# Tile 0's sums: two units joined onto others by VectorE, and queries of the last batch in other PSUM buffers

## The chip, the cores and the metric

The kernel runs on one core of a Trainium2 chip. Its engines run in parallel, each through its own queue of instructions in a fixed order: TensorE (matmuls, with PE and PEld as its rows in the profile: the matmuls and the weight loads), VectorE (DVE), ScalarE (ACT), GpSimd (POOL, which here also issues the gathers) and SyncE (SP, which issues plain transfers). The metric is the device time of one launch in microseconds, the median of several runs.

## The reference

One layer of graph attention over 16 batches of 1024 nodes with 512 features, float32 throughout. `adj` is a 1024 x 1024 matrix of zeros and ones, the same for all batches; a node attends to those nodes where its row is not zero.

```
h = jnp.maximum(_layernorm(x, axis=-1), 0.0)
q, k, v = (h @ W + b).reshape(b, n, 8, 64)      # for Wq, Wk, Wv
scores = jnp.einsum('bihd,bjhd->bhij', q, k) / 8 + where(adj == 0, -1e9, 0)
out = softmax(scores) @ v                       # per head
return x + out
```

Here the three projections are written as one line. Rows of `adj` differ much in how many ones they have: a few nodes have a great many neighbours, most have very few.

## The kernel before

**Tiles and units.** At the start the nodes are sorted by their number of neighbours and cut into 8 tiles of 128 nodes, so that all nodes of a tile have about as many. Tile 0 holds those with the most (11 slots each), tile 7 those with the fewest (2 slots). For every slot of a tile, a gather fetches one neighbour's K and V row for each of the 128 nodes into a ring of 23 places in SBUF (`gather`, line 1339 on GpSimd's queue; line 1337, on SyncE's, for a node's own row, which is plain). The slots of a tile are cut into units of up to four: `UNITS` lists 14 of them, as (tile, first slot, number of slots). Tile 0 has four: numbers 10 to 13, which are (0, 0, 4), (-1, 0, 4), (0, 4, 4) and (0, 8, 3). The second, with -1, holds pieces: further neighbours of the longest rows, spread over all 128 partitions; its queries are made by one matmul with the matrix `owner` (line 1326), and what it gives goes back to its rows through a matmul with `owner_t`.

**A unit's way.** VectorE multiplies K by the queries (line 1349) and reduces each head (1353); ScalarE takes the exponent (1357); V is multiplied by the weights, one slot on VectorE (1369) and the rest on ScalarE, head by head (1383, eight instructions a slot); then the slots of a unit are folded into the first (`fold`, 1388, on VectorE, some on GpSimd). Line numbers are those of the kernel before; the changed kernel's are some 10 higher.

**The sum over units.** In the tiles 1 to 7 the units of a tile are joined by VectorE (`join`, 1395). In tile 0 TensorE adds them up in PSUM (`add_up`, 1407: a matmul with the identity, or with `owner_t`; float32, two instructions a slot), but `PAIRED = (13,)` says that unit 13 is first joined onto unit 12 by VectorE. So TensorE sums the units 10, 11 and 12, each folded to one slot. VectorE then scales by the row sums (1443), `x` is added (1457) and GpSimd stores the rows (1460). The last batch is different: all its tiles but 7 are summed in PSUM, no slots are folded there, and it takes its tiles in another order (`LAST_ORDER`), tile 0 first.

**The rest of a batch.** Eight tiles of `x` are loaded, normalised (1087), turned by TensorE (1094, into the PSUM buffers `pht`), copied (1099), and projected (1105 the bias, 1107 the four matmuls, eight instructions): K and V into the PSUM buffers `pkv`, queries into `q`, two buffers of each kind. K and V are copied out and stored to HBM, from where the gathers of that batch read.

**What sets the order.** Every operation is listed with its engine, what it waits for and the buffers that it takes. `PLACES` gives each a number, by kind of batch (0, 1, 2, 3 for all the middle ones, next to last, last), and `ordered` puts each engine's queue in the order of these numbers, as far as buffers allow. A slot of the ring is given to a later gather when the last reader of what was in it is done (`touch` notes that reader).

Of the kernel before, what the change touches and what calls it, by code (L numbers as in the profile page):

```python
# [10 lines left out]
F32 = mybir.dt.float32  # L11
# [39 lines left out]
LAST_SHARES = (7, 6, 5, 4)  # L51
POOL_FOLDS = ((5, 0), (4, 0), (1, 0), (1, 4), (-1, 0))
# [67 lines left out]
        load_x=(31.049, 36.783, 44.902, 44.496, 48.208, 49.457, 50.746, 51.179,),  # L120
        norm=(67.626, 67.496, 74.201, 74.321, 77.427, 77.725, 77.636, 78.055,),
        flip=(54.462, 56.273, 60.803, 60.32, 67.659, 69.837, 67.669, 79.954,),
        unflip=(74.149, 74.341, 77.678, 77.688, 77.945, 88.353, 77.949, 88.373,),
        queries=(67.388, 82.797, 119.567, 126.815, 126.985, 142.131, 160.895, 166.215, 178.754,),
        gather=(79.658, 76.69, 82.341, 88.71, 96.247, 85.455, 130.077, 131.141, 97.49, 131.444, 131.207, 114.891,
# [3 lines left out]
        multiply=(44.958, 52.73, 91.409, 107.808, 127.369, 113.75, 131.901, 138.313, 148.456, 153.849, 160.505,  # L129
            168.689, 179.852, 179.155,),  # L130
        score=(44.978, 57.826, 94.048, 113.658, 128.337, 128.327, 144.151, 145.637, 148.577, 157.948, 166.105,
            172.449, 184.805, 190.24,),
        exponent=(110.192, 112.182, 112.945, 116.538, 127.025, 123.554, 131.068, 131.453, 148.261, 154.25, 165.903,
            171.356, 175.668, 179.424,),
        row_sums=(45.058, 64.344, 99.8, 117.62, 136.45, 158.731, 164.776, 202.291,),
        share=(52.255, 69.019, 106.586, 121.953,),
        weigh_v=(59.989, 136.42, 144.838, 146.315, 160.08, 162.684, 175.763, 179.21, 187.767,),
        weigh_s=(110.345, 112.764, 112.932, 112.883, 116.3, 116.059, 117.574, 119.959, 124.847, 119.535, 128.006,
            128.663, 128.577, 131.031, 143.069, 132.507, 147.11, 147.956, 133.383, 152.679, 153.798, 152.071, 165.883,
            155.205, 162.477, 175.658, 170.488, 167.365, 173.07, 174.582, 173.706, 178.014, 177.193, 176.615, 185.5,  # L140
            184.485, 184.518,),
        fold=(70.374, 102.858, 111.725, 138.272, 138.767, 136.852, 152.743, 144.2, 146.252, 146.283, 150.583, 159.412,
            156.722, 158.554, 164.711, 178.225, 172.057, 178.008, 186.564, 193.371, 186.442, 186.911, 194.742,
            203.514, 203.407, 203.544,),
        residual=(135.465, 136.054, 138.986, 147.406, 155.322, 174.928, 178.773, 223.099,),
        put_out=(135.561, 137.722, 153.06, 153.852, 172.277, 177.998, 210.259, 235.861,),
        join=(147.909, 162.67, 175.165, 205.718,),
        scale=(148.512, 165.374, 176.705, 210.064,),
        copy_q=(156.881,),
        add_up=(194.415, 206.93, 207.51,),  # L150
        more=(192.479,),
        pass_on=(194.778,),
        seen=(334.802,),
    ),
    1: dict(
        load_x=(-44.115, -43.713, -20.801, -33.74, -31.898, 35.921, 38.439, 40.768,),
        stats=(-68.353, -65.27, -59.298, -59.327, -16.301, -2.07, 22.869, 35.363,),
        norm=(-2.505, 0.857, 14.906, 21.095, 32.005, 25.638, 51.323, 59.514,),
        flip=(10.656, 11.218, 19.532, 62.497, 64.408, 64.772, 74.481, 81.456,),
        unflip=(1.813, 12.295, 17.709, 25.348, 35.031, 47.394, 57.982, 68.046,),  # L160
        proj_kv=(14.072, 17.322, 17.231, 42.55, 31.914, 64.021, 67.093, 64.398, 68.263, 71.481, 74.522, 77.094,
            77.939, 81.753, 84.619, 84.783,),
        evict_kv=(14.761, -27.097, 20.006, 23.587, 21.632, 43.531, 45.467, 32.738, 46.833, 59.822, 57.969, 60.522,
            69.174, 71.434, 72.595, 77.428,),
        store_kv=(7.044, 4.137, 13.698, 21.344, 43.631, 47.431, 47.421, 48.019,),
        variance=(-62.085, -59.298, 11.773, 41.168,),
        power=(-12.513, 19.605, 40.688, 54.482,),
        shift=(-59.504, -54.386, 26.781, 53.07,),
        queries=(94.739, 98.673, 106.104, 113.147, 115.672, 117.647, 123.411, 133.796, 173.926,),
        gather=(49.683, 84.791, 50.82, 87.832, 88.192, 50.603, 115.921, 116.04, 66.859, 116.49, 116.391, 116.11,  # L170
# [619 lines left out]
def pairs_up(b, B, u):  # L790

    return b < B - 1 and u in PAIRED

# [865 lines left out]
```

## Time and profile before

| | us |
|---|---|
| median of 3 runs | 1617.21 (1616.22 to 1619.01) |
| the profiled execution's own time | 1629.6 |
| its span, first to last instruction | 1627.9 |
| mean granted TensorE clock over the span | 0.987 |

The profiled execution is 12.4 us longer than the median. Times in a trace count from the span's start. A row of the timeline is a group of equal instructions on one engine; in square brackets stands how long the engine was idle before it and what ended that. VectorE and TensorE overlap the end of an instruction with the next, so what one costs is read from its start to the next one's start. The word "issue" means that the profile shows nothing that was waited for.

### The profile page before, as it was taken

How to read it: one execution, taken by the hardware profiler on the slowest of the kernel's cores; microseconds unless marked ns; L12 is line 12 of the kernel's file. 1: busy time of each engine (PE TensorE's matmuls, PEld its weight loads, DVE VectorE, ACT ScalarE, POOL GpSimd, SP SyncE). 2: the span in 40 equal slices, each digit the busy share in tenths (PEclk: the TensorE clock that was granted, in tenths of full speed). 3: DMA queues.
4: the chain of work that ended last, by engine and by line, in shares of the span. 5: the costliest groups of instructions: out<-in, count | busy, mean ns of one | idle time of the engine just before them, and what ended most of it. 6: DMA issues, size and time to landing. Idle time of an engine off the chain costs nothing.

```text
span 1627.9 us, 19217 instructions
## 1 busy us (share of the span) xinstructions
PE 1563.9 (96%) x4190; PEld 724.6 (45%) x4212; DVE 1531.8 (94%) x2090; ACT 1439.9 (88%) x5428; POOL 1275.3 (78%) x1185
## 2 busy tenths in 40 slices
PE   8889999999999999999999999999999999999688
PEld 4444444444444444444444444444444444444233
DVE  8679999999999999999999999999999999999897
ACT  4258989999998989899898989989899998989887
POOL 3766778788888888888888888888888878877785
PEclk9999999999999999999999999999999999999789
DMA  6487998999899998989999898999999899998895
GB/s 246 144 326 246 334 340 328 338 344 350 311 370 338 350 339 334 352 319 374 331 348 340 332 340 326 364 352 334 344 333 334 338 371 321 351 346 301 315 355 201
DMA packets 149875, 531.55 MB, mean 327 GB/s; under 512 B 19052, under 2 KB 19052, under 8 KB 149752
## 3 DMA queue, kind: packets, MB, share of 16 engines
q0 software_dynamic: 109840, 390.70, 65.8%
q1 hardware_dynamic: 39912, 139.56, 23.2%
q8 instruction: 35, 0.57, 0.1%
q14 instruction: 88, 0.72, 0.1%
HBM read 429.46 MB, written 100.72 MB: 326 GB/s over the span
## 4 chain that ended last, share of the span: by engine, by line
DVE 36%; ACT 15%; POOL 13%; issue 10%; PE 5%; DMA 3%; DVEq 0%; POOLq 0%; SPq 0%; ACTq 0%
ACT ring L1383 12%; DVE ring L1349 10%; DVE weights L1353 9%; DVE ring L1388 6%; POOL ring L1339 6%; PE acc L1407 2%; DVE st L1061 2%; POOL out_dram L1460 2%; POOL ring L1388 2%; PE pq L1107 2%; DMA ring<-kv,index 2%; DVE ring L1369 2%; POOL x L1457 1%; DVE ring L1395 1%; ACT kvt L1125 1%
## 5 line engine op out<-in xcount | busy, mean ns | idle before, releaser
L1383 ACT ACTIVATE ring<-ring,weights 128x64 f32<-128x64 f32 x4704 | 1155.0, 341 | 48.5 <-DVE weights L1362 24.5
L1339 POOL DMA_INDIRECT ring<-kv,index x608 | 650.1, 1069 | 183.1 <-issue 163.2
L1107 PE MATMUL pq<-wq,hT 128*128 128x512 f32 x1024 | 461.9, 594 | 0.7
L1107 PE MATMUL pv<-wv,hT 128*128 128x512 f32 x960 | 431.4, 592 | 0.9 <-ACT kvt L1125 0.9
L1107 PE MATMUL pk<-wk,hT 128*128 128x512 f32 x960 | 431.6, 592 | 0.6 <-ACT hT L1099 0.2
L1353 DVE TENSOR_REDUCE weights<-ring 128x32 f32<-128x2048 f32 (+2 forms) x224 | 423.0, 1894 | 1.2
L1349 DVE TENSOR_TENSOR ring<-ring,pq 128x2048 f32<-128x2048 f32 (+2 forms) x208 | 388.5, 1868 | 12.2 <-remote 6.4
L1107 PEld LDWEIGHTS pq<-wq,hT 128*128 128x128 f32 x1024 | 195.2, 191 | 225.6 <-issue 221.8
L1107 PEld LDWEIGHTS pv<-wv,hT 128*128 128x128 f32 x960 | 181.9, 190 | 216.0 <-issue 211.9
L1107 PEld LDWEIGHTS pk<-wk,hT 128*128 128x128 f32 x960 | 182.1, 190 | 207.9 <-issue 202.8
L1388 DVE TENSOR_TENSOR ring<-ring 128x512 f32<-128x512 f32 (+1 forms) x301 | 250.6, 845 | 6.0 <-issue 4.2
L1460 POOL DMA_INDIRECT out_dram<-x,perm x128 | 146.5, 1145 | 40.0 <-issue 24.1
L1052 POOL DMA_INDIRECT x<-in_x_dram,perm x128 | 133.1, 1039 | 36.2 <-issue 31.0
L1388 POOL TENSOR_TENSOR ring<-ring 128x512 f32<-128x512 f32 x90 | 116.1, 1291 | 5.9 <-DVE ring L1388 3.5
L1457 POOL TENSOR_TENSOR x<-x,o 128x512 f32<-128x512 f32 x64 | 81.9, 1280 | 23.1 <-DVE o L1443 21.9
L1087 ACT ACTIVATE h<-x,shift,rstd 128x512 f32<-128x512 f32 x120 | 94.2, 815 | 5.2 <-DVE shift L1077 4.3
L1357 ACT ACTIVATE weights<-weights 128x32 f32<-128x32 f32 (+2 forms) x224 | 48.7, 223 | 54.9 <-DVE weights L1353 51.9
L1369 DVE TENSOR_TENSOR ring<-ring,weights 128x512 f32<-128x512 f32 x143 | 95.4, 681 | 0.0
L1094 PEld LDWEIGHTS pht<-ident,h 128*128 128x128 f32 x512 | 62.9, 142 | 66.0 <-issue 52.6
L1099 ACT COPY hT<-pht 128x512 f32<-128x512 f32 x128 | 73.1, 574 | 14.1 <-remote 12.3
L1061 DVE BATCH_NORM_STATS2 st<-x 128x6 f32<-128x512 f32 x120 | 81.4, 679 | 2.7 <-DMA x<-in_x_dram,perm 2.7
L1094 PE MATMUL pht<-ident,h 128*128 128x128 f32 x512 | 74.6, 276 | 9.7 <-ACT h L1087 9.0
(241 smaller groups left out, 1115.1 us busy)
## 6 DMA issues: line engine op xcount, KB each, us to landing
ring<-kv SPq DMA_DIRECT2D x128, 512.0 KB
kv<-kvt SPq DMA_DIRECT2D x120, 512.0 KB
ring<-kv,index POOLq DMA_INDIRECT x608
ring<-in_adj_dram SPq DMA_DIRECT2D x8, 512.0 KB
x_first<-in_x_dram SPq DMA_DIRECT2D x8, 256.0 KB
x<-in_x_dram,perm POOLq DMA_INDIRECT x128
out_dram<-x,perm POOLq DMA_INDIRECT x128
wk<-in_L_gnn_Wk_dram SPq DMA_DIRECT2D x1, 1024.0 KB
```

The lines of the kernel that those rows point to most:

```text
L1052: nc.gpsimd.indirect_dma_start(out=X[n][:], out_offset=None, in_=x_rows, in_offset=on(ap=perm[:, t : t + 1], axis=0), element_offset=b * N * D
L1061: nc.vector.bn_stats(st, X[n])
L1094: nc.tensor.transpose(PH[n][:, c, :], hn[:, ts(c, P)], ident)
L1107: nc.tensor.matmul(pt, HT[n][:, c, :], W[name][:, c, :], start=(apart and c == 0), stop=(n != -NT and c == DC - 1))
L1339: nc.gpsimd.indirect_dma_start(out=G[i][:, s].rearrange("p j d -> p (j d)"), out_offset=None, in_=KV[b % len(KV)][:], in_offset=on(ap=inde ...
L1349: nc.vector.tensor_tensor(k, k, Q[b, t][:, None, :].to_broadcast([P, count, D]), ALU.mult)
L1353: nc.vector.tensor_reduce(weights[:, w, :], heads(G[i][:, :count, 0, :]), AX.X, ALU.add)
L1369: nc.vector.tensor_tensor(v, v, own.to_broadcast([P, n, H, HD]), ALU.mult)
L1383: nc.scalar.activation(v[:, h, :], v[:, h, :], AF.Identity, scale=weights[:, c + s, h : h + 1])
L1388: engine.tensor_tensor(v[:, 0:n], v[:, 0:n], v[:, first : first + n], ALU.add)
L1457: (nc.vector if residual_by_vector(b, B, t) else nc.gpsimd).tensor_tensor(rows, rows, add, ALU.add)
L1460: nc.gpsimd.indirect_dma_start(out=out_rows[t], out_offset=on(ap=perm[:, t : t + 1], axis=0), in_=X.pop(b * NT + TILES.index(t))[:], in_of ...
```

## The change

Three things change. `PAIRED` becomes a table: unit 10 is joined onto unit 12, and unit 12 onto unit 13, both by VectorE, in all batches but the last. TensorE then sums the units 11 and 13 only, so two in place of three. In the last batch queries of the tiles 0 and 1 go into the PSUM buffers of K and V, and those of the tiles 2 and 3 into the buffers of the turned tiles; before, all went into the two of `q`. And nearly all numbers in `PLACES` are new, apart from the setup and the first projections. A unit that is joined away keeps its first slot in the ring until that join, where unit 10's was free after its sum on TensorE.

```diff
+LAST_QUERIES = {0: 'pkv', 1: 'pkv', 2: 'pht', 3: 'pht'}
...
     3: dict(
...
-        join=(157.031, 175.397, 183.579, 209.406,),
+        join=(158.199, 174.732, 182.978, 204.245, 209.904,),
...
-        add_up=(196.008, 204.056, 216.943,),
+        add_up=(209.732, 226.555,),
...
-PAIRED = (13,)
+PAIRED = {10: 12, 12: 13}
...
-        q = ("q", b, t)
+        q = (bank_of(b, B, t), "q", b, t)
...
-        elif pairs_up(b, B, u):
-            add(("join", k), "DVE", weighed + earlier)
-            touch(k, [0], ("join", k))
-            touch(k - 1, [0], ("join", k))
-            plan.ops[plan.number["add_up", k - 1]][2].append(("join", k))
-            added = [("add_up", b * NU + v) for v in added_up(b, B, home)]
         else:
-            add(("add_up", k), "PE", weighed + ([before] if u != parts[0] else []), [acc])
+            for from_, ready in [one for one in paired if PAIRED[one[0] % NU] == u]:
+                add(("join", from_), "DVE", weighed + ready)
+                touch(from_, [0], ("join", from_))
+                touch(k, [0], ("join", from_))
+                weighed = [("join", from_)]
+            paired = [one for one in paired if PAIRED[one[0] % NU] != u]
+            if pairs_up(b, B, u):
+                paired = [(k, weighed)]
+                continue
+            sums_of = added_up(b, B, home)
+            add(("add_up", k), "PE", weighed + ([before] if u != sums_of[0] else []), [acc])
...
+def bank_of(b, B, t):
+
+    return LAST_QUERIES.get(t, "q") if b == B - 1 else "q"
...
-            Q[b, t] = ps_q.tile([P, D], F32, tag="q", name=f"pq_{b}_{t}")
+            bank = bank_of(b, B, t)
+            Q[b, t] = dict(q=ps_q, pkv=ps_kv, pht=ps_h)[bank].tile([P, D], F32, tag=bank, name=f"pq_{b}_{t}")
...
-            to = i - 1 if pairs_up(b, B, i % NU) else b * NU + parts_of(t)[0]
+            to = b * NU + (PAIRED[i % NU] if pairs_up(b, B, i % NU) else parts_of(t)[0])
```

Where it moves instructions is shown at two places. The first is tile 0's sum in a middle batch. On TensorE before (acc_0 is tile 0's sum; pk, pv, pq are projections of the tile whose number follows; pht a turned tile; p_more the pieces' row sums):

```order
L1107 MATMUL pv_7_8730<-wv,hT_7_8663 128x512 x4
L1407 MATMUL acc_0_8801<-ring,ident 128x512
...
L1107 MATMUL pv_6_8808<-wv,hT_6_8758 128x512 x4
L1422 MATMUL p_more_8816<-more_8702,owner_t 128x8
...
L1107 MATMUL pq_7_8819<-wq,hT_7_7864 128x512 x4
L1407 MATMUL acc_0_8801<-ring,owner_t 128x512
...
L1107 MATMUL pk_6_8897<-wk,hT_6_8758 128x512 x4
L1094 MATMUL pht_5_8907<-ident,h_5_8905 128x128 x4
L1407 MATMUL acc_0_8801<-ring,ident 128x512
```

and in the changed kernel, at the same place:

```order
L1117 MATMUL pv_7_8694<-wv,hT_7_8686 128x512 x4
...
L1117 MATMUL pv_6_8729<-wv,hT_6_8727 128x512 x4
...
L1117 MATMUL pq_7_8756<-wq,hT_7_7887 128x512 x4
L1433 MATMUL p_more_8802<-more_8764,owner_t 128x8
L1418 MATMUL acc_0_8831<-ring,owner_t 128x512
...
L1117 MATMUL pk_6_8868<-wk,hT_6_8727 128x512 x4
L1418 MATMUL acc_0_8831<-ring,ident 128x512
L1104 MATMUL pht_5_8913<-ident,h_5_8894 128x128 x4
```

The first sum is gone, the pieces' sum comes first, and the last sum stands straight behind a projection.

On VectorE at the same place before, from the fold of unit 13 ahead of tile 6's multiplication (L1349) to tile 0's scaling (L1443); L1395 is the join, L1353 the reduction to scores, L1429 a row sum:

```order
L1388 TENSOR_TENSOR ring<-ring 128x512
L1349 TENSOR_TENSOR ring<-ring,pq_6_8872 128x3x512
L1395 TENSOR_TENSOR ring<-ring 128x512
L1362 TENSOR_TENSOR weights<-weights,inv_7_8884 128x16
L1353 TENSOR_REDUCE weights<-ring 128x24
L1429 TENSOR_REDUCE sums_8882<-weights 128x8
L1433 RECIPROCAL inv_6_8926<-sums_8882 128x8
L1369 TENSOR_TENSOR ring<-ring,weights 128x512
L1362 TENSOR_TENSOR weights<-weights,inv_6_8926 128x24
L1443 TENSOR_TENSOR o_0_8930<-acc_0_8801,inv_0_8828 128x512
```

and now, from tile 7's reduction on (L1406 is the join, L1364 the reduction, L1399 a fold, L1380 the multiplication by weights):

```order
L1364 TENSOR_REDUCE weights<-ring 128x16
L1406 TENSOR_TENSOR ring<-ring 128x512
L1399 TENSOR_TENSOR ring<-ring 128x512
L1360 TENSOR_TENSOR ring<-ring,pq_6_8834 128x3x512
L1440 TENSOR_REDUCE sums_8899<-weights 128x8
L1444 RECIPROCAL inv_7_8901<-sums_8899 128x8
L1399 TENSOR_TENSOR ring<-ring 128x512
L1373 TENSOR_TENSOR weights<-weights,inv_7_8901 128x16
L1406 TENSOR_TENSOR ring<-ring 128x512
L1364 TENSOR_REDUCE weights<-ring 128x24
L1380 TENSOR_TENSOR ring<-ring,weights 128x512
L1440 TENSOR_REDUCE sums_8899<-weights 128x8
```

There are two joins for one, and tile 6's row sum (the last row) stands behind the multiplication by weights and not ahead of it.

The second place is the start of the last batch's attention. On TensorE before (pq_0, pq_1, pq_2 are the last batch's queries, acc_0_12797 the sum of the batch before, acc_0_12847 that of the last):

```order
L1107 MATMUL pq_0_12662<-wq,hT_0_12528 128x512 x4
L1422 MATMUL p_more_12668<-more_12660,owner_t 128x8
L1407 MATMUL acc_0_12797<-ring,ident 128x512
L1407 MATMUL acc_0_12797<-ring,owner_t 128x512
L1326 MATMUL pq_-1_12812<-q_15_12715,owner 128x512
L1407 MATMUL acc_0_12797<-ring,ident 128x512
L1407 MATMUL acc_0_12847<-ring,ident 128x512 x4
...
L1107 MATMUL pq_1_12852<-wq,hT_1_12496 128x512 x4
L1407 MATMUL acc_0_12847<-ring,owner_t 128x512 x4
...
L1107 MATMUL pq_2_12936<-wq,hT_2_12430 128x512 x4
```

and now:

```order
L1117 MATMUL pq_0_12708<-wq,hT_0_12476 128x512 x4
...
L1117 MATMUL pq_2_12742<-wq,hT_2_12423 128x512 x4
L1433 MATMUL p_more_12775<-more_12630,owner_t 128x8
...
L1117 MATMUL pq_1_12816<-wq,hT_1_12469 128x512 x4
L1337 MATMUL pq_-1_12822<-q_15_12714,owner 128x512
L1418 MATMUL acc_0_12854<-ring,owner_t 128x512
L1418 MATMUL acc_0_12854<-ring,ident 128x512
L1418 MATMUL acc_0_12902<-ring,ident 128x512 x4
L1418 MATMUL acc_0_12902<-ring,owner_t 128x512 x4
```

The queries of tiles 2 and 1 stand ahead of the last batch's first sum, where they stood behind it. On VectorE the same moment, before, from tile 0's first multiplication of the last batch to its score (L1353):

```order
L1349 TENSOR_TENSOR ring<-ring,pq_0_12662 128x4x512
L1388 TENSOR_TENSOR ring<-ring 128x512
L1429 TENSOR_REDUCE sums_12075<-weights 128x8
L1431 TENSOR_TENSOR sums_12075<-sums_12075,p_more_12668 128x8
L1433 RECIPROCAL inv_0_12765<-sums_12075 128x8
L1388 TENSOR_TENSOR ring<-ring 128x2x512
L1353 TENSOR_REDUCE weights<-ring 128x32
```

and now, from the row sums that stood in between:

```order
L1440 TENSOR_REDUCE sums_12084<-weights 128x8
L1442 TENSOR_TENSOR sums_12084<-sums_12084,p_more_12775 128x8
L1444 RECIPROCAL inv_0_12779<-sums_12084 128x8
L1399 TENSOR_TENSOR ring<-ring 128x512
L1360 TENSOR_TENSOR ring<-ring,pq_0_12708 128x4x512
L1364 TENSOR_REDUCE weights<-ring 128x32
```

The score follows its multiplication at once; the fold and the row sum stand ahead of both, the larger fold behind.

## Rows read from the trace of the kernel before

**Rows 1.** The page, part 1: busy us, share of the span, instructions, by engine.

```profile
PE 1563.9 (96%) x4190; PEld 724.6 (45%) x4212; DVE 1531.8 (94%) x2090; ACT 1439.9 (88%) x5428; POOL 1275.3 (78%) x1185
```

**Rows 2.** Timeline, TensorE: queries of tile 0's pieces, six batches apart.

```profile
743.79 1.02 PE L1326 MATMUL pq_-1_6152<-q,owner 128*128 128x512 f32 x2
...
1315.88 1.02 PE L1326 MATMUL pq_-1_10945<-q,owner 128*128 128x512 f32 x2
```

**Rows 3.** Stretches: from:to, length, busy us by engine, clock, DMA share, GB/s.

```profile
100.00:300.00 200.00, 192.76 (x516) 88.82 (x520) 188.60 (x260) 174.07 (x660) 145.06 (x137) 1.00 0.89 323
...
743.84:1315.93 572.09, 565.49 (x1521) 261.82 (x1526) 555.44 (x709) 532.83 (x2034) 472.54 (x427) 1.00 0.93 342
...
1507.58:1553.42 45.84, 25.48 (x56) 10.39 (x54) 39.11 (x38) 38.03 (x155) 32.89 (x28) 0.74 0.87 322
1553.42:1617.31 63.89, 63.89 (x150) 28.46 (x151) 57.94 (x64) 61.42 (x260) 45.39 (x45) 0.97 0.81 296
```

**Rows 4.** Waits, 743.84 to 1315.93: total us, times, longest.

```profile
DVE sums L1429 <- ACT weights L1357: 6.1, 6, 1.0
...
PE acc L1407 <- POOL ring L1388: 4.3, 6, 0.9
...
DVE shift L1077 <- POOL rstd L1073: 1.8, 3, 0.6
DVE ring L1395 <- POOL ring L1388: 1.7, 6, 0.3
DVE o L1443 <- issue: 1.6, 6, 0.3
```

**Rows 5.** Timeline, TensorE, tile 0's sum in a middle batch: start, length, instruction.

```profile
1063.74 1.13 PE L1407 MATMUL acc<-ring,owner_t 128*128 128x512 f32 x2 [0.91 <-POOL ring L1388]
...
1075.65 0.60 PE L1094 MATMUL pht<-ident,h 128*128 128x128 f32 x4
1076.08 1.02 PE L1407 MATMUL acc<-ring,ident 128*128 128x512 f32 x2
1076.94 0.38 PE L1105 MATMUL pq<-bias_parts,chosen 128*128 128x512 bf16 x1
```

**Rows 6.** Timeline, VectorE, the same batch.

```profile
1065.56 1.21 DVE L1349 TENSOR_TENSOR ring<-ring,pq 128x1024 f32<-128x1024 f32 x1
...
1072.34 0.68 DVE L1395 TENSOR_TENSOR ring<-ring 128x512 f32<-128x512 f32 x1
1072.94 0.16 DVE L1362 TENSOR_TENSOR weights<-weights,inv 128x16 f32<-128x16 f32 x1
...
1075.78 0.21 DVE L1429 TENSOR_REDUCE sums<-weights 128x8 f32<-128x32 f32 x1 [1.01 <-ACT weights L1357]
...
1077.14 0.69 DVE L1443 TENSOR_TENSOR o<-acc,inv 128x512 f32<-128x512 f32 x1 [0.27 <-issue]
...
1081.87 2.28 DVE L1349 TENSOR_TENSOR ring<-ring,pq 128x2048 f32<-128x2048 f32 x1
```

**Rows 7.** Timeline, SyncE's queue, the same batch: two tiles' own rows.

```profile
1064.89 0.80 SPq L1337 DMA_DIRECT2D ring<-kv  x2
```

**Rows 8.** The chain that ended last: a transfer of own rows, issue to landing.

```profile
1208.18 7.54 DMA ring<-kv
```

**Rows 9.** Timeline, TensorE, the last batch.

```profile
1553.42 6.33 PE L1407 MATMUL acc<-ring,ident 128*128 128x512 f32 x10 [8.83 <-ACT ring L1383]
1559.58 0.38 PE L1105 MATMUL pq<-bias_parts,chosen 128*128 128x512 bf16 x1
...
1563.23 3.60 PE L1407 MATMUL acc<-ring,owner_t 128*128 128x512 f32 x8
```

**Rows 10.** Timeline, VectorE, the last batch's first multiplication to the second unit's.

```profile
1543.48 0.69 DVE L1388 TENSOR_TENSOR ring<-ring 128x512 f32<-128x512 f32 x1 [2.65 <-issue]
...
1546.53 2.28 DVE L1353 TENSOR_REDUCE weights<-ring 128x32 f32<-128x2048 f32 x1
...
1549.93 2.28 DVE L1349 TENSOR_TENSOR ring<-ring,pq_-1_12812 128x2048 f32<-128x2048 f32 x1
```

**Rows 11.** Timeline, ScalarE, the last batch's first exponent.

```profile
1548.84 0.23 ACT L1357 ACTIVATE weights<-weights 128x32 f32<-128x32 f32 x1 [3.49 <-DVE weights L1353]
```

More of the change, by code (lines that the diff above doesn't have):

```diff
@@ L129 @@
[L129 to L147, printed above, removed]
@@ L154 @@
+        scale=(153.427, 160.007, 182.169, 221.914,),
+        copy_q=(160.489,),
+        add_up=(200.11, 204.453,),
+        more=(186.586,),
+        pass_on=(192.394,),
+        seen=(326.256,),
     ),
     1: dict(
[L156 to L159, printed above, removed]
@@ L167 @@
[L167 to L170, printed above, removed]
[3 rows of a table removed]
-        multiply=(99.447, 106.031, 113.782, 124.398, 147.886, 144.395, 150.08, 154.625, 164.449, 169.213, 169.369,
-            178.115, 183.375, 191.926,),
-        score=(103.818, 107.037, 121.82, 141.74, 149.288, 149.734, 154.724, 157.574, 167.151, 169.267, 170.491,
-            182.002, 191.719, 192.028,),
@@ new lines @@
+        power=(-27.83, 37.657, 53.519, 73.645,),
+        shift=(-62.679, -50.756, 16.305, 46.882,),
+        queries=(96.04, 97.197, 100.217, 100.298, 118.016, 118.026, 122.901, 129.472, 170.315,),
+        gather=(49.722, 85.439, 49.712, 92.725, 88.878, 40.197, 130.734, 119.12, 91.528, 131.17, 129.324, 130.801,
[3 rows of a table added]
+        multiply=(97.646, 105.465, 117.719, 136.145, 147.976, 147.737, 154.978, 156.653, 158.632, 169.388, 171.311,
+            184.95, 187.823, 191.374,),
+        score=(104.805, 108.124, 118.759, 140.985, 148.529, 149.443, 155.805, 157.452, 163.849, 171.275, 177.068,
+            186.685, 188.087, 192.312,),
@@ new lines @@
+        power=(-14.991, -10.265, 52.087, 75.445,),
+        shift=(-30.12, -10.7, 53.88, 71.152,),
+        queries=(91.566, 91.576, 95.948, 105.026, 137.748, 142.356, 153.47, 158.033, 178.403,),
+        gather=(79.888, 96.164, 80.341, 100.314, 104.174, 78.277, 116.916, 113.956, 80.484, 124.104, 116.979, 105.307,
[3 rows of a table added]
+        multiply=(100.961, 103.766, 117.132, 135.054, 138.706, 139.368, 143.565, 149.08, 159.633, 172.002, 176.008,
+            179.546, 182.64, 188.483,),
+        score=(101.009, 105.353, 128.377, 135.874, 142.578, 140.199, 151.469, 151.102, 162.118, 173.01, 176.394,
+            181.922, 183.495, 191.159,),
@@ new lines @@
+        power=(-16.248, 13.193, 24.813, 75.905,),
+        shift=(-17.537, 12.061, 24.405, 64.603,),
+        queries=(105.553, 114.967, 117.853, 134.981, 139.088, 142.596, 149.894, 152.407, 164.897,),
+        gather=(76.982, 100.773, 71.893, 102.244, 104.263, 71.941, 117.648, 105.093, 80.672, 118.798, 113.462,
[3 rows of a table added]
+        multiply=(102.859, 110.919, 120.256, 121.594, 127.606, 133.289, 137.421, 146.803, 158.772, 168.658, 175.921,
+            177.499, 182.661, 185.356,),
+        score=(108.79, 114.812, 121.35, 125.982, 136.236, 136.795, 145.913, 152.286, 162.65, 171.648, 176.816,
+            182.615, 185.052, 189.96,),
@@ L378 @@
+        more=(158.123,),
+        pass_on=(211.725,),
+        seen=(547.64,),
     ),
```

393 lines of the change are left out of this document (196 added, 197 removed), and 37 rows, old and new, of the table gather.

## The prediction

> **What bounds the kernel now.** I read the page's busy times first, then the stretches, the period of a batch, the waits, and the timelines at the two places that the change touches. The page alone shows four engines close to full [rows 1], so the stretch of even running decides. In it the single matmul of tile 0's pieces returns after 572.09 us for six batches, 95.35 us a batch [rows 2]. Over the same stretch TensorE is busy 565.49 us, VectorE 555.44, ScalarE 532.83 and the DMA engines 0.93 of the time, at the full granted clock of 2.4 GHz [rows 3]. By sixths: TensorE 94.25 us busy and 1.10 idle; VectorE 92.57 busy and 2.78 idle; ScalarE 88.81 busy. TensorE is the first limit and VectorE the second, with little between them.
>
> What is in the idle time? TensorE's has 0.72 us a batch before the sum of the pieces' unit, which waits for GpSimd's fold (4.3 us in 6 times); 0.38 is scattered. VectorE's has four waits that come back in most batches: 1.02 for an exponent ahead of a row sum, 0.30 for GpSimd's power, 0.28 for GpSimd's fold ahead of a join, 0.27 ahead of tile 0's scaling: 1.87 [rows 4]. The other 0.91 are gaps under 0.15 us, between most instructions, and I count them as part of its work.
>
> The end is another regime. From 1507.58 to 1553.42 us no engine is full (TensorE 25.48 of 45.84), at a mean clock of 0.74; from 1553.42 to 1617.31 TensorE is busy without a gap, ScalarE 61.42 of 63.89, VectorE 57.94 [rows 3].
>
> **The joined units, even running.** TensorE loses one sum of one slice, two matmul instructions: from 1076.08 to the next instruction at 1076.94, 0.86 us a batch [rows 5]. VectorE gains one join of 128x512: from 1072.34 to the next at 1072.94, 0.60 us [rows 6]. Nothing hides either, since both engines are full; so this is a trade, and the later of two sums counts:
>
> - TensorE: 94.25 - 0.86 = 93.39 us of work. The wait for GpSimd's fold stays: TensorE comes to it 0.86 earlier, but GpSimd's fold now stands ahead of a gather that it stood behind. With the old 1.10 idle: 94.49.
> - VectorE: 92.57 + 0.60 + 0.91 = 94.08 us of work and short gaps. Of its waits two should go by the order. Tile 6's row sum stood directly behind the reduction that its exponent needs, and waited 1.01 us [rows 6]; now a multiplication by weights stands between (0.60), and in ScalarE's new order one copy out of PSUM less is ahead of that exponent. Tile 0's scaling came 0.2 us after the last sum ended; now the sum can end before 1076 and a fold stands ahead of the scaling. The two waits for GpSimd, 0.58 together, I leave: 94.66.
>
> The last two cannot both be had without some new waiting between three queues that run in order, so I take 94.8, nearer to VectorE's 94.66 than to today's 95.35: 0.55 us a batch. From 300 us to 1507.58 are 12.7 batches, say 13: 7.2 us. The ends: no gain beyond TensorE's 0.86, that is 11.2 us; and at worst VectorE keeps all four waits: 94.08 + 1.87 = 95.95, a loss of 0.60 a batch, 7.8 us.
>
> **New waits of this part.** There are three. First, TensorE's last sum waits for the second join, behind which stand all projections of the next batch. On VectorE the join begins 6.78 us after tile 7's multiplication at 1065.56 now [rows 6]; the new order puts the added join and a small multiplication of weights ahead of it, 0.69 us, so it ends near 1073.7. TensorE reaches the sum near 1075.65 - 0.86 = 1074.8 [rows 5]: a reserve of 1.1 us, where today it is 3.1. From 1.1 us on TensorE stands, and from 1.9 on its saving is used up. Second, the first unit's slot of the ring stays taken until its join. Before, TensorE's sum of that unit freed it; tile 4's own rows of the next batch go there, and SyncE issued them with another tile's at 1064.89 [rows 7]. Now they wait for the first join, which by the order lies about midway between tile 7's multiplication and the second join, near 1069.7. Such a transfer took 7.54 us in the chain [rows 8]: landing 1077.2. The multiplication that needs it stands at 1081.87 today [rows 6], about 1081.2 then (0.60 more, two waits of 1.02 and 0.27 less). Cost nothing, with 4.0 us in hand. Third, the slot of the third unit comes free with its join near 1073.7 rather than with the sum at 1076.94, so the gather behind it on GpSimd's queue is freer than now.
>
> **The last queries.** Projections of tiles 2 and 1 move in front of the wait in which TensorE has little to do, since they need no buffer of the two that queries share. One takes from 1559.58 to 1563.23, 3.65 us [rows 9]; two are 7.3 us off the busy run from 1553.42. VectorE and ScalarE do not shrink with it. ScalarE has 2.47 us of idle time in that run [rows 3], so this alone can give at most about that. The order adds a thing: tile 0's first score of the last batch now stands straight behind its multiplication. Before, it stood behind folds of the batch before that waited 2.65 us and more [rows 10], and ScalarE stood 3.49 us for it [rows 11]. Ends for the last stretch: nothing, and 2.47 + 3.49 = 5.96. The gathers of the second unit still have to land, VectorE began it without a wait at 1549.93, so I take the middle, 3 us.
>
> **The new places elsewhere.** Nearly all places of all batches are new numbers, and the order is reshuffled by a few positions on each queue. In the first 300 us TensorE idles 7.24 us between 100 and 300 [rows 3]; half of that either way is my bound, and I take zero.
>
> **Sum.** 7.2 + 3.0 = 10.2 us. The profiled execution took 1629.6 us, with a span of 1627.9 and 1.7 around it: 1619.4. The median of the runs, 1617.2, lies 12.4 lower; less the same 10.2 it is 1607.0.
>
> **Rivals.**
>
> 1. VectorE eats the gain. Its waits shrink only to 1.26, then 94.08 + 1.26 is today's period; only the end gains: 1614. For it: VectorE has 0.91 less to spare than TensorE had. Against: the 1.02 us wait visibly loses its cause.
> 2. VectorE becomes the limit and keeps its waits, because the join ahead of the second fold pushes everything behind it and TensorE stands at its last sum: 95.95 a batch, 7.8 lost and 3 won, 1622. It decides at the second join of a batch, from about 1.9 us later than I place it.
> 3. Tile 4's own rows come late. It begins where the transfer takes over 11.5 us. One microsecond late makes VectorE's batch 95.66, 4 us in all, 1618; three late 1644. Against it: 7.54 in the row.
> 4. TensorE is not a limit at all, its busy time being that of overlapping instructions; then VectorE is, at 97 of 100, and each join costs its 0.60, fifteen of them 9.0, with nothing won at the end: 1626. Against it: matmuls start 0.43 us apart with no gap wherever the timeline is opened, and TensorE's waits are few [rows 4, 5].
>
> The Trainium skill, Perfetto Trace Analysis, section Identifying the Most-Contended Engine, speaks for this fourth case: it calls matmul busy time a poor measure of TensorE, because matmuls are pipelined, and would have the weight loads' share read instead, while VectorE's busy share is fair as it stands. By that rule TensorE has half its time free (weight loads 261.82 of 572.09 us [rows 3]) and the change loads the fuller engine: 1626. The trace does not bear that out, as a weight load of 0.17 us goes with each matmul of some 0.38 us, so that its share cannot pass about 46% here however full TensorE is.
>
> **Chances.** My forecast 0.61, its own range 1600 to 1613; the first rival 0.16; the second 0.12; the third 0.06; the fourth 0.05. A difference of 0.2%, 3.2 us, is what a measurement of this kernel can tell from none: faster means under 1614.0, slower over 1620.4. The first rival lies at the border and gives most of "same", with part of the third: 0.16. Slower takes the second, the fourth, the rest of the third and a little for places that I have not followed: 0.22. Faster: 0.62. The range runs from the best of both main terms with nothing from the start, 1617.2 - 11.2 - 5.96 = 1600, a microsecond lower for the start, to the second rival, 1622.
>
> **What would show it.** The period between the single matmuls of tile 0's pieces near 94.8 us; TensorE busy 93.4 a batch; VectorE 93.2 busy with under 1 us in waits over 0.15, and the row sum's wait gone. At TensorE's last sum of a batch no wait for VectorE's join. Between the last projection and the first sum of the last batch, three projections of queries and not one; ScalarE's 3.49 us gone. I am wrong if the period is 95.3 or more, if VectorE waits for rows of K and V in the middle of the run, or if the gain sits in the first 300 us.

## The result and the profile after

The changed kernel takes 1600.15 us, the median of 6 runs (1597.45 to 1602.04); the kernel before takes 1615.72 in the same comparison. The ratio is 0.9902, with a 95% interval of 0.9887 to 0.9917: 15.6 us (13 to 18) faster. The forecast was 10.2 us, in the right direction and too small.

The profiled execution after took 1597.45 us, 2.7 under its median, with a span of 1595.8. That of before lay 12.4 over its median. The two spans differ by 32 us, twice what the medians do, so no difference of whole spans is used here; stretches that start and end at the same instruction are. The busy times, to be read against [rows 1]:

```profile
PE 1548.5 (97%) x4151; PEld 719.2 (45%) x4182; DVE 1532.9 (96%) x2105; ACT 1437.5 (90%) x5428; POOL 1257.0 (79%) x1185
```

The period, from TensorE's timeline, by the same instruction and the same batches as [rows 2]:

```profile
726.30 1.02 PE L1337 MATMUL pq_-1_6123<-q,owner 128*128 128x512 f32 x2
...
1285.36 1.02 PE L1337 MATMUL pq_-1_10917<-q,owner 128*128 128x512 f32 x2
```

559.06 us for six batches: 93.18 a batch, where it was 95.35. The stretches that answer to [rows 3] (length, then busy us of PE, PEld, DVE, ACT, POOL, clock, DMA share, GB/s); the third row runs from the last batch's first query projection to 1.1 us ahead of the row with its first sum, the fourth from there to the end. The last two rows of [rows 3] have other ends, so their lengths are not to be compared with these:

```profile
100.00:300.00 200.00, 195.88 (x528) 90.31 (x530) 196.67 (x267) 181.37 (x690) 153.52 (x142) 1.00 0.92 331
726.34:1285.36 559.02, 557.86 (x1502) 260.31 (x1513) 547.40 (x715) 532.39 (x2039) 464.56 (x426) 1.00 0.96 350
1496.78:1523.40 26.62, 14.18 (x34) 5.86 (x32) 26.21 (x26) 25.28 (x105) 19.40 (x18) 0.79 0.90 331
1523.40:1595.80 72.40, 60.92 (x138) 25.81 (x139) 62.85 (x79) 60.73 (x258) 45.96 (x46) 0.92 0.71 271
```

In the even run TensorE stands 1.2 us in 559; before it stood 6.6 in 572. VectorE is busy 91.2 us a batch, 1.3 less than before, although it has a join more. The waits of that stretch (total, times, longest) are these, to be read beside [rows 4]: VectorE's, then TensorE's only one.

```profile
DVE x L1468 <- POOL ring L1399: 3.1, 6, 1.6
DVE shift L1087 <- POOL rstd L1083: 2.5, 4, 0.6
DVE ring L1360 <- PE pq L1117: 0.3, 1, 0.3
DVE o L1454 <- PE acc L1418: 0.2, 1, 0.2
```

```profile
PE pq_-1_6922 L1337 <- DVE ring L1360: 0.4, 1, 0.4
```

The waits for the exponent and for GpSimd's fold ahead of a sum or a join are gone, and so is that ahead of tile 0's scaling, but for one of 0.2 us. A wait for GpSimd's fold ahead of tile 4's residual (the addition of `x`) is new. Tile 0's sums in one batch on TensorE, and on VectorE from tile 7's multiplication to the scaling, answering to [rows 5, 6]:

```profile
1040.62 1.10 PE L1418 MATMUL acc<-ring,owner_t 128*128 128x512 f32 x2
...
1052.51 1.02 PE L1418 MATMUL acc<-ring,ident 128*128 128x512 f32 x2
```

```profile
1042.57 1.22 DVE L1360 TENSOR_TENSOR ring<-ring,pq 128x1024 f32<-128x1024 f32 x1
...
1046.27 0.68 DVE L1406 TENSOR_TENSOR ring<-ring 128x512 f32<-128x512 f32 x1
...
1050.14 0.69 DVE L1406 TENSOR_TENSOR ring<-ring 128x512 f32<-128x512 f32 x1
...
1053.01 0.20 DVE L1440 TENSOR_REDUCE sums<-weights 128x8 f32<-128x32 f32 x1
...
1054.18 0.69 DVE L1454 TENSOR_TENSOR o<-acc,inv 128x512 f32<-128x512 f32 x1
```

No bracket stands on any of them. The second join ends at 1050.83 and TensorE comes to its sum at 1052.51, 1.7 us later; I had placed 1.1.

Where did VectorE's 1.3 us come from? Two groups of small instructions hold it: the variance (L1070, after L1080) and the sharing out of the weights (L1362, after L1373). First before, from 743.84 to 1315.93, then after, six batches each (busy us, mean ns of one):

```profile
L1070 DVE TENSOR_SCALAR rstd<-mv 128x2 f32<-128x2 f32 x24 | 10.0, 417 | 0.0
L1362 DVE TENSOR_TENSOR weights<-weights,inv 128x24 f32<-128x24 f32 (+2 forms) x24 | 9.1, 377 | 0.4
```

```profile
L1080 DVE TENSOR_SCALAR rstd<-mv 128x2 f32<-128x2 f32 x24 | 4.7, 195 | 0.0
L1373 DVE TENSOR_TENSOR weights<-weights,inv 128x24 f32<-128x24 f32 (+2 forms) x24 | 4.4, 181 | 0.6
```

The same work costs 10.0 us less in six batches, 1.67 a batch. A mean hides the cause: of the 24 variances before, 18 took 0.14 us on average and 6, one a batch, 1.25. Each of the six stood beside GpSimd's fold and ended 0.04 us after it. One of them, VectorE's row, then GpSimd's:

```profile
1062.46 1.25 DVE L1070 TENSOR_SCALAR rstd<-mv 128x2 f32<-128x2 f32 x1
```

```profile
1062.41 1.27 POOL L1388 TENSOR_TENSOR ring<-ring 128x512 f32<-128x512 f32 x1
```

Of the 24 sharings before, 7 took 0.5 us or more, the others at most 0.26. Each of the seven stood beside an addition of `x` on GpSimd (L1457) and ended some 0.06 us after it:

```profile
1090.32 0.51 DVE L1362 TENSOR_TENSOR weights<-weights,inv 128x32 f32<-128x32 f32 x1
```

```profile
1089.48 1.29 POOL L1457 TENSOR_TENSOR x<-x,ring 128x512 f32<-128x512 f32 x1
```

In the new order no variance stands beside a fold on GpSimd and the longest took 0.30 us, the longest sharing 0.19. The Trainium skill, SBUF — State Buffer, section Who interferes with whom, names a pair of SBUF ports that VectorE and GpSimd share and that, for certain instructions, one of them holds for a whole instruction. These rows agree with that, a block to the end of GpSimd's instruction and not a slowdown.

The last batch, TensorE from its first query projection on, answering to [rows 9]; then ScalarE's first two exponents, answering to [rows 11], and the second of them before:

```profile
1496.78 0.38 PE L1115 MATMUL pq<-bias_parts,chosen 128*128 128x512 bf16 x1
...
1500.43 0.38 PE L1115 MATMUL pq<-bias_parts,chosen 128*128 128x512 bf16 x1
...
1504.21 0.38 PE L1115 MATMUL pq<-bias_parts,chosen 128*128 128x512 bf16 x1
...
1513.38 2.08 PE L1418 MATMUL acc<-ring,owner_t 128*128 128x512 f32 x2 [4.50 <-DMA ring<-kv,index]
1524.50 6.80 PE L1418 MATMUL acc<-ring,ident 128*128 128x512 f32 x10 [9.04 <-issue]
1531.14 3.63 PE L1418 MATMUL acc<-ring,owner_t 128*128 128x512 f32 x8
```

```profile
1518.44 0.23 ACT L1368 ACTIVATE weights<-weights 128x32 f32<-128x32 f32 x1 [1.06 <-DVE weights L1364]
...
1526.62 0.23 ACT L1368 ACTIVATE weights<-weights 128x32 f32<-128x32 f32 x1 [2.03 <-DVE weights L1364]
```

```profile
1555.55 0.23 ACT L1357 ACTIVATE weights<-weights 128x32 f32<-128x32 f32 x1 [0.60 <-DVE weights L1353]
```

Three projections stand ahead of the batch's first sum at 1524.50, as forecast. ScalarE's wait of 3.49 shrank to 1.06, but the second grew from 0.60 to 2.03, so the two together lost only 1.0. Counted from the end of the last K and V projection, the first exponent comes 4.4 us earlier than before, the second 2.9 and the end 6.1: about half of what the tail gains lies behind these two exponents.

### The profile page after: what moved, and what is told of

Read it like the earlier page. It is cut to its first block, busy times and chain, and to the rows that moved or that the text cites. A ratio compares the mean times of both kernels' runs of the same rounds, so it can differ in the third digit from the quotient of the medians.

```text
span 1595.8 us, 19282 instructions
## 1 busy us (share of the span) xinstructions
PE 1548.5 (97%) x4151; PEld 719.2 (45%) x4182; DVE 1532.9 (96%) x2105; ACT 1437.5 (90%) x5428; POOL 1257.0 (79%) x1185
## 4 chain that ended last, share of the span: by engine, by line
DVE 39%; PE 22%; ACT 12%; POOL 10%; issue 9%; DMA 7%; DVEq 0%; POOLq 0%; SPq 0%; ACTq 0%
DVE ring L1360 11%; DVE weights L1364 10%; ACT ring L1394 9%; DVE ring L1399 6%; DMA ring<-kv,index 6%; PE pk L1117 5%; PE pv L1117 5%; PE pq L1117 5%; POOL ring L1350 4%; DVE ring L1380 3%; DVE st L1071 2%; PE pv_first L1117 2%; PE pk_first L1117 2%; POOL ring L1399 2%; POOL x L1062 1%
## 5 line engine op out<-in xcount | busy, mean ns | idle before, releaser
L1350 POOL DMA_INDIRECT ring<-kv,index x608 | 618.0, 1016 | 185.5 <-issue 159.7
L1364 DVE TENSOR_REDUCE weights<-ring 128x32 f32<-128x2048 f32 (+2 forms) x224 | 422.2, 1890 | 0.9
L1360 DVE TENSOR_TENSOR ring<-ring,pq 128x1536 f32<-128x1536 f32 (+2 forms) x208 | 388.7, 1869 | 4.6 <-DMA ring<-kv,index 4.0
L1399 DVE TENSOR_TENSOR ring<-ring 128x512 f32<-128x512 f32 (+1 forms) x301 | 253.0, 856 | 2.7 <-ACT ring L1394 2.1
L1471 POOL DMA_INDIRECT out_dram<-x,perm x128 | 151.3, 1182 | 38.1 <-issue 24.4
L1062 POOL DMA_INDIRECT x<-in_x_dram,perm x128 | 142.3, 1111 | 34.0 <-issue 27.6
L1399 POOL TENSOR_TENSOR ring<-ring 128x512 f32<-128x512 f32 x90 | 116.1, 1299 | 10.0 <-DVE ring L1399 8.3
L1380 DVE TENSOR_TENSOR ring<-ring,weights 128x512 f32<-128x512 f32 x143 | 105.8, 747 | 1.3 <-ACT weights L1368 1.0
L1135 ACT COPY kvt<-pk 128x512 f32<-128x512 f32 x120 | 69.4, 578 | 7.8 <-PE pk L1117 7.8
```

Of the source, the lines that this page charges most:

```text
L1062: nc.gpsimd.indirect_dma_start(out=X[n][:], out_offset=None, in_=x_rows, in_offset=on(ap=perm[:, t : t + 1], axis=0), element_offset=b * N * D
L1350: nc.gpsimd.indirect_dma_start(out=G[i][:, s].rearrange("p j d -> p (j d)"), out_offset=None, in_=KV[b % len(KV)][:], in_offset=on(ap=inde ...
L1360: nc.vector.tensor_tensor(k, k, Q[b, t][:, None, :].to_broadcast([P, count, D]), ALU.mult)
L1364: nc.vector.tensor_reduce(weights[:, w, :], heads(G[i][:, :count, 0, :]), AX.X, ALU.add)
L1380: nc.vector.tensor_tensor(v, v, own.to_broadcast([P, n, H, HD]), ALU.mult)
L1399: engine.tensor_tensor(v[:, 0:n], v[:, 0:n], v[:, first : first + n], ALU.add)
```

## The experiments

Two measures are used. The ratio is against the kernel before on the same chip (its median was 1615.3 in the first four runs, 1622.5 and 1621.5 in the next two fours); the changed kernel's is 0.9902. The table gives what the traces show: *period*, by the pieces' query matmuls of six batches of the even run, as above; *14 batches*, from the first batch's to the 15th's; *tail*, from the end of the last K and V projection to the end. lastq_only has before's code in the even run, and 95.97 for 95.35: in the old order a period of one trace is known to some 0.6, and smaller differences are read from the ratio. What differs between these two traces is VectorE, busy 560.48 us in lastq_only's six batches (below) and 555.44 before, not TensorE, 565.56 and 565.49 [rows 3]:

```profile
731.80:1307.63 575.83, 565.56 (x1520) 262.07 (x1525) 560.48 (x709) 533.22 (x2034) 470.16 (x427) 1.00 0.92 339
```

The same work took VectorE 5.0 us longer, and the six batches 3.7 longer, which speaks for VectorE's time counting in the old order. In all nine traces with the old order six of 24 variances took over 1.2 us and three to seven sharings over 0.4; in the five with the new places none did, with the old pairing or the new.

| kernel | ratio (95%) | period | 14 batches | tail |
|---|---|---|---|---|
| before | 1 | 95.35 | 1326.9 | 104.9 |
| changed | 0.9902 (0.9887 to 0.9917) | 93.18 | 1317.5 | 98.8 |
| pair_only | 1.0062 (1.0049 to 1.0076) | 95.36 | 1328.3 | 111.6 |
| places_only | 1.0012 (1.0003 to 1.0022) | 94.12 | 1336.4 | 99.4 |
| lastq_only | 1.0023 (1.0011 to 1.0034) | 95.97 | 1329.5 | 106.2 |
| no_last_q | 1.0006 (0.9996 to 1.0016) | 93.25 | 1317.6 | 115.3 |
| pair_late_sum | 1.0062 (1.0049 to 1.0074) | 95.66 | 1329.5 | 111.7 |
| before_late_sum | 0.9990 (0.9980 to 1.0000) | 95.00 | 1324.7 | 104.6 |
| after_pe_more | 0.9953 (0.9939 to 0.9967) | 93.87 | 1328.2 | 99.1 |
| after_dve_more | 0.9936 (0.9923 to 0.9949) | 93.50 | 1321.3 | 99.1 |
| before_var_early | 1.0029 (1.0019 to 1.0039) | 95.47 | 1329.2 | 104.3 |
| pair_var_early | 1.0112 (1.0082 to 1.0143) | 96.04 | 1331.6 | 114.1 |
| before_dve_more | 1.0040 (1.0027 to 1.0053) | 95.80 | 1329.1 | 105.3 |
| tail_after | 1.0629 (1.0615 to 1.0643) | 97.43 | 1428.4 | 100.2 |

**The parts one at a time.** Four kernels, each with a part of the change.

pair_only, in the places of each middle kind of batch (kind 3 shown), with no last queries:

```
-        join=(157.031, 175.397, 183.579, 209.406,),
+        join=(157.031, 175.397, 183.579, 203.9, 209.406,),
-        add_up=(196.008, 204.056, 216.943,),
+        add_up=(204.056, 216.943,),
-PAIRED = (13,)
+PAIRED = {10: 12, 12: 13}
```

> The kernel before with the new pairing alone: unit 10 is joined onto 12 and 12 onto 13, TensorE sums two units a batch; places and last queries are those of before, the added join stands right behind the fold of unit 12. Theory A (the pairing carries the gain, TensorE being the limit): a period of 94.5 us or less between the single matmuls of tile 0's pieces, 7 to 11 us faster than before, 1605 to 1609. Theory B (the new places carry it, the pairing being only a trade): VectorE keeps its waits and gets 0.60 us more a batch, a period of 95.3 to 96.0, 1615 to 1624.

Slower (1624.5), with theory B's period, but not by theory B's sum. The even run did not move: TensorE is busy 0.7 us a batch less, and stands that much longer. Its wait for GpSimd's fold grew from 4.3 us in six batches [rows 4] to 5.8. The stretch of these six batches, and that wait:

```profile
733.00:1305.10 572.10, 561.41 (x1508) 259.82 (x1514) 557.66 (x715) 532.88 (x2035) 471.73 (x427) 1.00 0.93 342
```

```profile
PE acc L1419 <- POOL ring L1400: 5.8, 6, 1.7
```

Most of what it lost lies in the tail (111.6 for 104.9). GpSimd's timeline there shows a gather of the last batch that stands over 10 us for the first join of tile 0 in the batch before, since unit 10's slot comes free only then, and VectorE's shows the pieces' multiplication late for its rows:

```profile
1538.72 0.96 POOL L1351 DMA_INDIRECT ring<-kv,index  x1 [10.26 <-DVE ring L1407]
```

```profile
1545.53 2.29 DVE L1361 TENSOR_TENSOR ring<-ring,pq_-1_12812 128x2048 f32<-128x2048 f32 x1 [7.08 <-DMA ring<-kv,index]
```

places_only, kind 3 shown:

```
-        join=(158.199, 174.732, 182.978, 204.245, 209.904,),
+        join=(158.199, 174.732, 182.978, 209.904,),
-        add_up=(209.732, 226.555,),
+        add_up=(198.0, 209.732, 226.555,),
-PAIRED = {10: 12, 12: 13}
+PAIRED = {12: 13}
```

> The changed kernel with the old pairing: unit 12 is joined onto 13, TensorE sums the units 10, 11 and 13; places and last queries are the changed kernel's, the added sum stands behind unit 10's fold and ahead of the pieces' sum. Theory A: TensorE gets its 0.86 us a batch back, a period of 93.18 + 0.86 = 94.04 or more, 11 to 13 us slower than the changed kernel, 1611 to 1613. Theory B: at most 3 us slower than the changed kernel, 1600 to 1603, and most of the distance to the kernel before remains.

Slower than either theory gave, but the total is no fair price of the places: the added sum stood badly where I put it in two batches outside the even run (3.9 and 4.2 us of waiting for unit 10's fold). The period is fair, and shows both: 95.35 to 94.12 by the places, on to 93.18 by the pairing. TensorE is nearly full there:

```profile
735.60:1300.30 564.70, 563.06 (x1514) 262.87 (x1525) 546.14 (x710) 531.45 (x2036) 471.02 (x427) 1.00 0.94 347
```

So in the old places the pairing is worth nothing a batch, as far as one trace tells, and in the new ones 0.94 us.

lastq_only:

```
+LAST_QUERIES = {0: 'pkv', 1: 'pkv', 2: 'pht', 3: 'pht'}
-        queries=(275.407, 263.498, 261.178, 220.533, 211.109, 194.523, 156.874, 106.462, 148.456,),
+        queries=(275.407, 263.498, 261.178, 220.533, 211.109, 106.47, 148.455, 106.462, 148.456,),
```

> The kernel before with the last batch's queries in the idle PSUM buffers, those of tiles 2 and 1 projected ahead of the last batch's first sum; nothing else changed. If the early projections carry the gain of the tail (the tail of the changed kernel is 6.1 us shorter in the traces): 3 to 6 us faster than before, 1610 to 1613, no queries between the first two sums of the last batch. Rival (VectorE's order of the first score carries it, ScalarE's wait of 3.49 us stays here): within 2 us of before, 1614 to 1617.

The rival, and a little slower than it gave. Early projections alone bring nothing.

no_last_q:

```
-LAST_QUERIES = {0: 'pkv', 1: 'pkv', 2: 'pht', 3: 'pht'}
+LAST_QUERIES = {}
-        queries=(271.812, 271.184, 263.729, 223.275, 211.729, 117.864, 177.125, 114.617, 177.135,),
+        queries=(271.812, 271.184, 263.729, 223.275, 211.729, 211.725, 196.71, 114.617, 177.135,),
```

> The changed kernel with all last queries in the two buffers of before, those of tiles 1 and 2 behind the first and the third sum of the last batch, as before. If the early projections carry the gain of the tail: 3 to 6 us slower than the changed kernel, 1603 to 1606, with the period of the even run unchanged at 93.2. Rival: within 2 us of it, 1599 to 1602.

Neither: some 15 us slower, all of it in the tail (115.3 for 98.8), with the even run as in the changed kernel. With two buffers only, TensorE's queue stops at a projection until VectorE has read an older tile's queries, and VectorE stops at tile 0's scaling for a sum that stands behind that projection:

```profile
1551.12 0.61 PE L1115 MATMUL pq<-bias_parts,chosen 128*128 128x512 bf16 x1 [7.61 <-DVE ring L1360]
```

```profile
1560.42 0.69 DVE L1454 TENSOR_TENSOR o<-acc,inv 128x512 f32<-128x512 f32 x1 [7.04 <-PE acc L1418]
```

Two projections stand here where I put them; another position might cost less.

**Is it TensorE's wait?** One place moved: the pieces' sum one projection later, in the pairing alone and in the kernel before. The edit of pair_late_sum (that of before_late_sum changes the same number):

```
-        add_up=(204.056, 216.943,),
+        add_up=(206.955, 216.943,),
```

> The kernel with the new pairing alone, and one place more: in the middle batches TensorE's sum of the pieces' unit stands behind the projection of tile 6's queries instead of ahead of it. Theory C (with the old places the removed sum of 0.86 us turned into a longer wait of TensorE for GpSimd's fold, 1.78 us a batch for 0.72): the wait goes, the period falls from 95.36 to 93.6 to 94.5, and the time to 1606 to 1616. Rival (VectorE's waits hold the period, TensorE's wait is only where the slack shows): 95.3 still, 1622 to 1626.

> The kernel before with that one place alone (three sums, old pairing). Theory C: the wait of 0.72 us a batch goes, a period of 94.5 to 94.8, 6 to 9 us faster than before, 1606 to 1610. Rival: 95.3, within 2 us of before, 1613 to 1618.

In both kernels that wait for GpSimd's fold is gone. With the pairing the period stayed, and TensorE waits elsewhere, for buffers of queries that VectorE has yet to read:

```profile
PE pq L1116 <- DVE ring L1361: 4.0, 11, 0.8
```

So theory C falls for the pairing: TensorE's wait was where the slack showed, not the cause. In the kernel before the same edit gained 0.1% (0 to 0.2%) in time, 1.6 us and not 6 to 9.

**Which engine is the limit?** An instruction more a batch, on either engine:

```
                 nc.tensor.matmul(Q[b, t], owner, Q0[b], start=True, stop=True)
+                if b < B - 1:
+                    nc.tensor.matmul(Q[b, t], owner, Q0[b], start=True, stop=True)
```

> The changed kernel with the matmul of the pieces' queries done twice in all batches but the last (same operands, same result): two instructions more on TensorE a batch, 0.86 us by the start-to-start cost of such a pair. If TensorE is the limit now (idle 0.17 us a batch): period 94.0, 11 to 14 us slower than the changed kernel, 1611 to 1614. If VectorE is (idle 2.0): at most 3 us, 1600 to 1603.

The period rose by 0.69, which is what 0.86 leaves when the idle 0.17 is used up. The time rose by 0.51% (0.9953 for 0.9902), 8 us, less than forecast. In six batches TensorE never stands:

```profile
735.20:1298.40 563.20, 563.20 (x1526) 262.71 (x1525) 547.55 (x715) 532.25 (x2038) 467.58 (x426) 1.00 0.94 347
```

On VectorE, `tensor_mul` of tile 0's scaling stands twice, in the changed kernel and in the kernel before:

> The changed kernel with tile 0's scaling done twice in all batches but the last (same operands, same result): one 128x512 instruction more on VectorE a batch, 0.6 us. If TensorE is the limit and VectorE has 1.1 us a batch beyond its short gaps: within 3 us of the changed kernel, 1598 to 1603, the period at 93.2 to 93.4. If VectorE is the limit: 0.6 a batch, 9 us slower, 1608 to 1611.

> The kernel before with tile 0's scaling done twice in all batches but the last (same operands, same result): 0.6 us a batch more on VectorE. Theory D: VectorE's time counts in full, a period of 95.8 to 96.0, 7 to 9 us slower than before. If TensorE alone is the limit of the kernel before: within 3 us of before, the period at 95.4.

In the changed kernel five of the six batches take 93.0 to 93.5 and one 95.0, and the time rises by 0.34%, 5.5 us: not free, but not the 0.6 a batch of a limit. In the kernel before the time rises by 0.40%, 6.5 us of the 9 that theory D gave (the period by 0.45). There VectorE's time counts for the most part. The two times are known to 2 to 3 us each, so they do not tell the two kernels apart. What does is TensorE, which has hardly any idle time left in the changed one. An instruction more on TensorE was not tried in the kernel before.

**Does the stretched variance count?**

```
-        variance=(-23.408, 4.462, 9.386, 61.65,),
+        variance=(-23.408, 3.95, 9.386, 61.65,),
```

> The kernel before with one VectorE instruction of 128x2 elements (the variance of one pair of tiles, line 1070) one row statistic earlier in the middle batches, so that it ends before GpSimd's fold begins; in the trace of before it stood beside that fold once a batch and took 1.25 us instead of 0.14. Theory D (VectorE with its waits sets the old period, and this stretch is 1.1 us of it): the period falls from 95.35 to 94.3 to 94.9, 5 to 10 us faster than before. Rival (the stretch only fills time that VectorE would wait in): 95.2 or more, within 2 us of before.

> The new pairing with the old places, and that same instruction one row statistic earlier. Theory D: TensorE's work is 0.86 us a batch less here, so the relief of VectorE shows in full: the period falls from 95.36 to 94.2 to 94.5, 10 to 13 us faster than the pairing alone (which was 0.6% slower than before), 0 to 4 us faster than before. Rival: 95.2 or more, still 0.5% slower than before.

The edit did the opposite of what it was for: the variance came while a gather was running on GpSimd with the fold straight behind it, and took 1.93 us, to the fold's end. VectorE's row, then GpSimd's:

```profile
1059.15 1.93 DVE L1070 TENSOR_SCALAR rstd<-mv 128x2 f32<-128x2 f32 x1
```

```profile
1058.82 0.94 POOL L1339 DMA_INDIRECT ring<-kv,index  x1 [0.30 <-issue]
1059.77 1.28 POOL L1388 TENSOR_TENSOR ring<-ring 128x512 f32<-128x512 f32 x1
```

That still doses the cause, upwards: 0.68 us more of stretch a batch. Over 11 middle batches that is 7.5 us. With the pairing the period rises by 0.68, from 95.36 to 96.04, and the ratio by 0.5%, 8 us, known to some 5 and with 2.5 of it in the tail. In the even run VectorE's time thus counts in full there. Without the pairing the ratio rises by 0.3%, 4.7 us. But in that trace the sharings took less than before, 6.7 us in six batches for 9.1, and the variances 14.6 for 10.0: a net dose of 0.37 us a batch, 4.1 us in all. So this may be in full too. Shortening the stretch in the old places was not tried.

**The tail in another state.** tail_after has pair_only's places to the 14th batch and the changed kernel's behind, with `LAST_QUERIES`.

> The new pairing with the old places up to the 14th batch, and the changed kernel's places and last queries in the last two batches; four instructions at the seam stand where the buffers let them. If the places of the last two batches with the early queries give the tail its gain (99.2 us from the last batch's first query projection to the end before, 105.8 with the pairing alone, 93.6 in the changed kernel): 94 to 95 us here, 10 to 12 us faster than the pairing alone, so within 3 us of before. If the tail's gain comes from the state in which the even run reaches it: 99 us or more, at most 6 us faster than the pairing alone.

The seam ruined the time (the batches around it took 107.5, 162.5 and 117.6 us; the first of them is in the table's period), so the total says nothing. The tail itself was 100.2 us, by the measure of the expectation 94.6, behind an even run of quite another kind. That speaks for the tail's gain being the last two batches' own: their places together with the early queries. It is not proof, since the seam changed the state in which the tail began. The other traces agree: four kernels with before's last two batches have tails of 104.3 to 105.3, four with the changed kernel's 98.8 to 99.4. Either part without the other has 106 or more, in no_last_q with two projections that may stand badly.

## Why the prediction was right in direction and short in size

- **The even run, 0.55 us a batch forecast, 2.17 measured.** The step that failed is VectorE's term: 92.57 of work, 0.60 for the join and 0.91 of short gaps, 94.08, taken as a floor. The join was priced well, but 92.57 was not fixed work: it held 1.67 us a batch in which small instructions stood blocked by GpSimd, and the new places moved them. VectorE ended at 91.2 with the join. TensorE then became the limit (after_pe_more), and the pairing brought 0.94, near the 0.86 of the removed sum. By the traces the new places are worth 1.23 a batch (places_only). That they owe it to the blocked instructions rests on the doses above; the same places also took away VectorE's wait of 1.02 and TensorE's of 0.72, and what each of these brought was not measured apart.
- **TensorE's old idle time of 1.10, kept in the sum.** It fell to 0.19 (by the starts of its matmuls, see below, from 1.6 to 0.3). I had left the wait for GpSimd's fold standing; the pieces' sum in the new order starts when the fold is long done.
- **VectorE's waits.** Two were to go and two to stay. The row sum's and the scaling's went, as argued from the order. GpSimd's fold ahead of a join went too; its power stayed (2.5 us in six batches, 1.8 before); tile 4's residual brought 0.3 a batch and 1.6 once.
- **13 batches at the even rate.** Wrong, to the other side. Nine batches, from the fourth matmul of pieces' queries to the 13th, gained 16.9 us; the fourteen together only 9.4 in the two traces, 12.0 against lastq_only, which has before's code up to the last batch. The batches at either end run by other places and gave back the difference (the second took 105.6 us for 90.7, the 13th 101.6 for 95.4). That the forecast of 7.2 us lies as near as it does is luck: a rate four times too small, over batches of which some lost.
- **The new waits.** None came, as costed: the last sum has 1.7 us in hand; no multiplication of the even run waits for tile 4's own rows. The held slot does cost something where I did not look: in the last batch, with the old places, 7 us of tail.
- **The last queries, 3 us forecast, 6.1 measured** (104.9 to 98.8), beyond the upper end of 5.96 by a hair. The mechanism was at most half right: ScalarE's first wait shrank by 2.4, its second grew by 1.4. And I priced the projections and the order as two terms that add, and they do not: either alone makes the tail longer.
- **The start, taken as nothing.** Up to the fourth matmul of pieces' queries the changed kernel is 1.5 to 2.0 us ahead of pair_only and lastq_only (445.3 for 446.8 and 447.3), within the bound of 3.6. At the first of these matmuls it was 4.1 and 4.8 ahead. The 9.4 us of the fourteen batches and the 6.1 of the tail already make up the 15.6 measured; what the time ahead of them adds is not known, since it differs by up to 13 us between traces of the same start (last section).
- **The rivals.** VectorE eats the gain: exactly what pair_only did in the even run, 95.36 for 95.35, so without the new places this rival would have come in. VectorE with all waits (95.95): of the kernels with the new pairing only pair_var_early came to it, and tail_after by its seam. Late rows of tile 4: not in the even run. TensorE not a limit: refuted for the new order by after_pe_more; in the old one 0.86 us less on TensorE brought nothing (pair_only, 1624.5), much as this rival had it.

TensorE's busy time fell by 1.3 us a batch in the even run (565.49 to 557.86 in six) and not by 0.86. Its work did not: with each matmul priced from its start to the next one's where nothing is waited for (0.43 us for a float32 instruction of 128x512, 0.22 for one of a bias), and with the 6 and 12 bias matmuls that the two traces lack, it went from 562.5 to 557.3, 0.86 a batch. The rest is drawing: a matmul is shown 0.59 us long, so one that stands ahead of a wait counts 0.16 of that wait as busy, and there are fewer waits. What stays open is which of the new places moved the collisions; they were changed together.

## What to carry to other kernels

Before an engine's busy time is taken as its work, look at its small instructions for a spread: a 128x2 instruction that takes 0.14 us in 18 cases and 1.25 in 6 is a wait inside a busy bar, and an order can remove it. When two engines are within 2% of each other, their busy shares do not tell which sets the period: here TensorE had the larger share, and taking 0.86 us from it brought nothing in the old order and 0.94 a batch in the new one. Price such a trade on both, with one instruction more on each. Buffers, order and joined slots interact at the end of a program: parts that help together can each cost when tried alone.

## What the runs showed of the hardware that was not expected

A 128x2 VectorE instruction that came 0.33 us after the start of a GpSimd gather, with a fold straight behind the gather, lasted to the end of the fold: 1.93 us instead of 0.14, in all twelve cases of two kernels. Beside gathers alone it took at most 0.37 us. The other way round, of 24 gathers that took over 1.4 us in the six batches before (0.96 is the median), 23 ended 0.81 to 0.82 us after the end of a VectorE TENSOR_TENSOR that had run beside them. Many others beside such an instruction took 1.0 us or less, so overlap alone is not enough; what more it takes was not tried. The time until the first matmul of the pieces' queries was 168.9 us in lastq_only and 180.6 in the profiled execution before, whose code is the same up to the last batch: that is most of the 12 us by which the profile of before lay over its median. In the nine traces with the old order this time lies between 168.2 and 181.5 us.
